# Two-layer graph network on one core: dilation loads and comparison re-staggered, ends of the second network's layers cut into smaller steps

## The chip, the cores and the metric

The kernel runs on 1 core of a Trainium2 chip. The core has five instruction streams, each in order: TensorE (PE; its weight loads are shown as PEld), VectorE (DVE), ScalarE (ACT), GpSimd (POOL) and SyncE (SP, which here only issues DMAs). The metric is device time in microseconds (us), lower is better. Before the change the median of three runs is 2877.07 us (2874.56 to 2882.93).

## The reference, cut to what matters

There are 16 graphs of 1024 nodes with 128 features, and a dense symmetric weight matrix `adj` per graph. Two networks are applied in turn, each to relu(layernorm(x)), and each result is added to x.

```python
# first network, three layers of
h = h @ W + b
nh = h / max(norm(h), eps)
h = (adj * (nh @ nh.T)) @ h          # relu between layers

# second network
keep = dilate(adj > 0)               # for n in range(1024): one row after the other
#   num = row.sum(); sf = (num + 1) // 2 if num > 10 else 1
#   rm = row & (cumsum(row) % sf == 0); row n and column n lose rm
adj_d = adj * keep
# three layers of
agg = (adj_d @ x) / deg
out = agg @ Wr + x @ Wx + b
h = batchnorm(relu(out / norm(out)))  # statistics over all 16 graphs
# at the end
y = concat(h1, h2, h3) @ Wl + bl
```

Two things order the work. The dilation is sequential in rows. A batch norm of the second network needs every graph's result before any graph may enter the next layer.

## The kernel before, in words

**Stage A (about the first 1700 us): the first network, with the dilation beside it.** `layer0()` is a generator that emits the first network for pairs of graphs. For each row of 128x128 blocks, `Batch.products` (line 329) multiplies features with features into a PSUM tile `pg`, of which there are two (line 344), and VectorE multiplies `pg` by the block's weights into `ew` (lines 353 and 356). TensorE then transposes `ew` (line 373) and sums it with the features (lines 384 and 398). The natural blocks of `adj` come from DRAM into `nat` (two buffers, line 245) and are transposed by TensorE (line 260); the rest of a block row goes straight into `adjA` (line 253). Both are DMAs on SP's queue.

`dilation()` (line 545) is a second generator. A block is a group of 128 rows (index k) of half the graphs: BH = 8 patterns, one for each graph. `dilate` makes three generators for a block:

- `loads` (line 581): for each pattern, SP loads 128 rows of `adj` (tile `an`, two buffers, line 585). ScalarE makes a 0/1 pattern of them (lines 587 and 588). For k > 0, SP also loads what is kept of the earlier columns, transposed (tile `kl`, two buffers, line 591), and VectorE combines the two (line 594).
- `rounds` (line 621): a fixed number of small iterations, which finds for every row which ranks go.
- `scans` (line 725): for each pattern, VectorE's running sum gives ranks (line 740, tile `rank`, three buffers), ScalarE takes an absolute value of them in place (line 749), VectorE compares them with a radius (line 760, tile `kp`), and GpSimd's queue stores the result to DRAM (line 761).

The loads of the next block are emitted between the scans of the present one. The main loop (line 797) hands out pieces of `layer0` according to weights that the dilation yields. That makes a program order; the framework's scheduler then sorts each engine's instructions by priority in that order and its own estimates of readiness, and the engines run what it wrote in order. So an edit of the dilation also shifts neighbouring instructions of the first network.

At about 1569 us a branch (line 822) tests whether the fast dilation was exact; it is not taken here. The rest of the first network follows, up to about 1700 us.

**Stage B (about 1700 to 2140 us): the second network's first layer.** It masks `adj`, writes the masked matrix back to DRAM, and sums.

**Stage C (about 2140 us to the end): its layers 1 and 2, and the output.** For each graph, `start2` (line 1065) normalizes (`normed`, line 1050: one ScalarE instruction over 1024 columns), projects with Wr and Wx (`weighted`, line 848), and projects the layer before with its part of Wl into `acc` (`project`, line 1057). `Sums.add` then does the large sums (line 888). `norms` (line 926) makes the row norms of half a graph: four squares on ScalarE with a sum each (line 933), a root and a reciprocal (`inv_root`, line 152), and one scaling on GpSimd (line 938). `keep` (line 942) transposes the scaled half and adds it to the batch norm's statistics. After the last graph comes `batchnorm` (line 950), and no graph can enter the next layer before it. `residual` (line 1075) folds x and the output bias into `acc`. The output loop (line 1113) projects the last layer and writes the sum.

Of the kernel before, what the change touches and what calls it, by code (L numbers as in the profile page):

```python
# [9 lines left out]
F16 = mybir.dt.float16  # L10
I32 = mybir.dt.int32
AF = mybir.ActivationFunctionType
ALU = mybir.AluOpType
# [3 lines left out]
P = 128  # L17
# [29 lines left out]
def tile_adj_preln_d2(  # L47
# [152 lines left out]
    with ExitStack() as actx:  # L200
# [362 lines left out]
        def dilate(k, half, exact):  # L563
# [6 lines left out]
            def pattern(i):  # L570
                return patt[:, (at0 + i) % SLOTS, :]
# [7 lines left out]
            E = radius = shift = low = None  # L579

            def loads():
                for i in range(BH):
                    b = half * BH + i
                    an = poold.tile([P, N], F32, tag="an", name=f"an{nk}_{i}")
                    nc.sync.dma_start(an, adj[b, cols, :])
                    on = pattern(i)[:, 2 + k * P :]
                    nc.scalar.activation(on, an[:, k * P :], AF.Sign)
                    nc.scalar.activation(on, on, AF.Relu, accum_out=rest[:, i : i + 1])
                    if k:
                        pk = poold.tile([P, NCH - 1, P], F16, tag="kl", name=f"kl{nk}_{i}")  # L590
                        nc.sync.dma_start(
                            pk[:, :k, :].rearrange("p j q -> p (j q)"), keep_d[b][: k * P, cols], transpose=True
                        )
                        nc.vector.scalar_tensor_tensor(
                            pattern(i)[:, 2 : 2 + k * P],
                            an[:, : k * P],
                            0.0,
                            pk[:, :k, :].rearrange("p j q -> p (j q)"),
                            ALU.is_gt,
                            ALU.mult,  # L600
                            accum_out=left[:, i : i + 1],
                        )
# [122 lines left out]
            def scans():  # L725

                i = 0
                while i < BH:
                    at_ = (at0 + i) % SLOTS
                    n = min(BH - i, SLOTS - at_)  # L730
                    here = patt[:, at_ : at_ + n, diag]
                    nc.vector.tensor_tensor(here, here, E[:, i : i + n, :], ALU.subtract)
                    i += n
                ranks = {}
                for i in range(BH + 1):
                    if i < BH:

                        pt = pattern(i)
                        ranks[i] = rank = poold.tile([P, N], F16, tag="rank", bufs=3, name=f"rank{nk}_{i}")
                        nc.vector.tensor_tensor_scan(rank, pt[:, 1 : N + 1], pt[:, 2:], 0.0, ALU.add, ALU.add)  # L740
                        yield True, 2.5
                    if i == 0:
                        continue

                    i -= 1
                    b = half * BH + i
                    pt, rank = pattern(i), ranks.pop(i)
                    tc.keep_in_program_order(
                        nc.scalar.activation(  # L749
                            rank, rank, AF.Abs, bias=shift[:, i : i + 1], scale=1.0 if exact else -1.0  # L750
                        )
                    )
                    kp = poold.tile([P, N], F16, tag="kp", name=f"kp{nk}_{i}")
                    if exact:
                        nc.vector.tensor_scalar(
                            kp, rank, low[:, i : i + 1], radius[:, i : i + 1], ALU.max, ALU.not_equal
                        )
                        nc.vector.tensor_tensor(kp, kp, pt[:, 2:], ALU.is_ge)
                    else:
                        nc.vector.tensor_scalar(kp, rank, radius[:, i : i + 1], None, ALU.not_equal)  # L760
                    nc.gpsimd.dma_start(keep_d[b][cols, :], kp)
                    yield False, 0.8

# [17 lines left out]
        step0()  # L781
        batches[1].fetch()

        mi = pool1.tile([P, P], I32, tag="mi", name="mi")[:NB, :]
        nc.gpsimd.dma_start(mi, nodemask.rearrange("b (c p) -> (b c) p", p=P))
        mfl = pool1.tile([P, P], F32, tag="up", name="mfl")[:NB, :]
        nc.vector.tensor_copy(mfl, mi)
# [49 lines left out]
    with ExitStack() as bctx:  # L837
# [29 lines left out]
        class Sums:  # L867
# [55 lines left out]
                        ALU.add,  # L923
                    )

            def norms(self, h):

                nm, b = f"{self.l}_{self.b}_{h}", self.b
                hc = slice(h * CPH, (h + 1) * CPH)
                ss = pool2.tile([P, CPH], F32, tag="in_ss", name=f"ss_{nm}")  # L930
                for c in range(CPH):
                    n = h * CPH + c
                    nc.scalar.activation(  # L933
                        self.own[:, n, :], self.o[:, n, :], AF.Square, accum_out=ss[:, c : c + 1]
                    )
                rn = inv_root(pool2, ss, nm)
                nc.vector.tensor_tensor(rn, rn, mf[:, b, hc], ALU.mult)  # L937
                nc.gpsimd.tensor_tensor(  # L938
                    self.o[:, hc, :], self.o[:, hc, :], rn.unsqueeze(2).to_broadcast([P, CPH, D]), ALU.mult
                )  # L940

            def keep(self, h):

# [21 lines left out]
        with kctx, ExitStack() as c1:  # L965
# [42 lines left out]
            def follow():  # L1008
                nonlocal last
                s, q, aT = behind.pop(0)  # L1010
                s.add(q, aT)
                if q == CPH + 1:
                    s.norms(0)
                if q == NCH - 1:
                    s.norms(1)
                    last = s

            then = ahead1
# [30 lines left out]

        def normed(l, b, ab):  # L1050
            hT = pool2.tile([P, NCH, P], F32, tag="hT2", name=f"hT2_{l}_{b}")
            nc.scalar.activation(  # L1052
                hT.rearrange("p c q -> p (c q)"), hR[:, b, :], AF.Identity, bias=ab[:, 1:2], scale=ab[:, 0:1]
            )
            return hT

        def project(l, b, hT):

            for h in range(NHALF):
                pp = ps_sm.tile([P, CPH, P], F32, tag="sm", name=f"pp_{l}_{b}_{h}")  # L1060
                for c in range(CPH):
                    nc.tensor.matmul(pp[:, c, :], lhsT=hT[:, h * CPH + c, :], rhs=wl[:, l, :], start=True, stop=True)  # L1062
                yield h, pp, acc[:, b, h * CPH : (h + 1) * CPH, :]

        def start2(l, b):
            hT = normed(l, b, ab)
            got = Sums(l, b, hT, CPH, 0, ps_a)
            for h, pp, a in project(l - 1, b, hT):
                if l == 1:
                    nc.scalar.activation(a, pp, AF.Copy)  # L1070
                else:
                    nc.vector.tensor_tensor(a, pp, a, ALU.add)
            return got

        def residual(b):

# [9 lines left out]
        for l in (1, 2):  # L1086
            last = None
            then = start2(l, 0)
            for b in range(B):
                now = then  # L1090
                for q in range(NCH):
                    aT = row_of(q, f"{l + 1}_{b}")
                    nc.sync.dma_start(aT, adT_d[b][q])
# [11 lines left out]
                        now.norms(0)  # L1105
                    if q == NCH - 2 and b == B - 1:
                        now.keep(0)
                now.norms(1)
                last = now
            last.keep(1)  # L1110
            ab = batchnorm(l)

        for b in range(B):
            y = pool2.tile([P, NCH, D], F32, tag=("o", "own")[b % 2], name=f"y_{b}")
# [66 lines left out]
```

## Time and profile before

| | us |
|---|---|
| median of three runs | 2877.07 |
| the profiled execution's own time | 2874.98 |
| its span, first to last instruction | 2873.2 |
| TensorE busy | 2659.3 (93% of the span) |
| VectorE busy | 1939.7 (68%) |
| ScalarE busy | 1426.0 (50%) |
| GpSimd busy | 473.7 (16%) |
| mean granted TensorE clock | 0.981 |

The profile is one execution. A line such as `PE pg L344 <- DVE ew L356: 63.5, 51, 3.8` means that TensorE's instructions of line 344, which write `pg`, were late 51 times, 63.5 us in total and 3.8 us at the longest, and that a VectorE instruction of line 356 ended the wait. In a list in order of time, the first number is the start, the second the duration, and a bracket holds the idle time of that engine before it and what ended it. A matmul with 32-bit operands is recorded as two matmuls.

### The profile page before, as it was taken

The page shows a single profiled execution, that of the slowest core. Times are in us where ns is not written, and L with a number is a line of the kernel's source. Part 1 is how long each engine was busy: PE and PEld are TensorE (multiplying, and loading weights), DVE is VectorE, ACT ScalarE, POOL GpSimd, SP SyncE. Part 2 cuts the span into 40 slices and gives each one's busy share as a digit, 9 for nine tenths or more (in the row PEclk, how much of TensorE's full clock was granted, in tenths as well). Part 3 has the DMA queues.
Part 4 walks back from the last instruction along what each step waited for, and adds up shares of the span by engine and source line. Part 5 has one row for each costly group of instructions (what it writes and reads, how often), then busy time and mean ns, then how long its engine had stood idle before and what let it go on. Part 6 is the DMA issues. An engine that isn't in the chain of part 4 may idle for free. (4 is left out here: it accounts for less than half of the span.)

```text
span 2873.2 us, 51953 instructions
## 1 busy us (share of the span) xinstructions
PE 2659.3 (93%) x18803; PEld 2199.0 (77%) x18803; DVE 1939.7 (68%) x4913; ACT 1426.0 (50%) x4100; POOL 473.7 (16%) x619
## 2 busy tenths in 40 slices
PE   6999998999999998989998998999989999899997
PEld 4666666666666666666676778898879999899996
DVE  3778778778878778789877467677762333356565
ACT  6767557557556556556455333333333433333334
POOL 3112112112011111112111012222220010010102
PEclk9999999999999999999999999999999999999998
DMA  9447247248366476286253249999985665577764
GB/s 287 130 139 236 77 155 236 86 137 247 87 186 178 99 199 191 80 257 191 55 190 115 75 168 380 379 401 401 397 333 191 202 213 202 183 236 229 237 230 134
DMA packets 382233, 585.22 MB, mean 204 GB/s; under 512 B 85200, under 2 KB 266448, under 8 KB 381968
## 3 DMA queue, kind: packets, MB, share of 16 engines
q1 hardware_dynamic: 343280, 425.28, 47.2%
q0 software_dynamic: 38688, 156.53, 14.5%
q8 instruction: 151, 2.47, 0.4%
q14 instruction: 114, 0.93, 0.1%
HBM read 403.44 MB, written 163.58 MB: 197 GB/s over the span
## 5 line engine op out<-in xcount | busy, mean ns | idle before, releaser
L888 PE MATMUL agg<-hw,aT 128*128 128x128 f32 (+1 forms) x6144 | 744.4, 277 | 8.2 <-DVE aT L985 7.3
L888 PEld LDWEIGHTS agg<-hw,aT 128*128 128x128 f32 x6144 | 713.6, 193 | 13.4 <-DVE aT L985 9.7
L344 PE MATMUL pg<-nhT 128*128 128x512 f32 (+3 forms) x1152 | 460.2, 502 | 69.5 <-DVE ew L356 65.5
L384 PE MATMUL po<-ew,hS 128*128 128x512 f32 (+3 forms) x1152 | 458.4, 501 | 8.7 <-ACT hTo L407 5.4
L356 DVE TENSOR_TENSOR ew<-pg,adjA 128x768 f32<-128x768 f32 (+3 forms) x528 | 423.2, 825 | 5.8 <-PE pg L344 5.7
L398 PEld LDWEIGHTS po<-ew,hS 128*128 128x128 f32 x2688 | 338.4, 193 | 40.3 <-issue 37.8
L398 PE MATMUL po<-ew,hS 128*128 128x128 f32 x2688 | 365.3, 277 | 1.2 <-ACT ew L374 1.2
L374 ACT ACTIVATE ew<-gt 128x512 f32<-128x512 f32 (+1 forms) x480 | 209.2, 465 | 247.8 <-PE gt L373 237.6
L344 PEld LDWEIGHTS pg<-nhT 128*128 128x128 f32 x1152 | 189.0, 194 | 164.8 <-issue 120.9
L740 DVE TENSOR_TENSOR_SCAN rank<-patt 128x1024 f16<-128x1024 f16 x128 | 295.0, 2316 | 0.9
L384 PEld LDWEIGHTS po<-ew,hS 128*128 128x128 f32 x1152 | 197.9, 195 | 100.8 <-issue 66.4
L373 PEld LDWEIGHTS gt<-ident,ew 128*128 128x128 f32 x1344 | 168.3, 143 | 100.2 <-issue 72.1
L353 DVE TENSOR_TENSOR ew<-pg,adjA 128x128 f32<-128x128 f32 x384 | 107.6, 280 | 184.9 <-PE pg L344 142.8
L938 POOL TENSOR_TENSOR o<-o,rn 128x512 f32<-128x512 f32 x96 | 111.4, 1160 | 646.6 <-DVE rn L937 627.7
L373 PE MATMUL gt<-ident,ew 128*128 128x128 f32 x1344 | 212.7, 276 | 4.9 <-PEq L822 2.4
L860 PE MATMUL pw<-wrx,hT 128*128 128x256 f32 x768 | 179.5, 388 | 10.5 <-ACT hT L1052 9.7
L862 DVE TENSOR_TENSOR own<-pw,bs 128x256 f32<-128x256 f32 x192 | 81.3, 424 | 156.9 <-ACT hw L861 156.8
L860 PEld LDWEIGHTS pw<-wrx,hT 128*128 128x128 f32 x768 | 145.0, 194 | 32.6 <-ACT hT L1052 10.5
L933 ACT ACTIVATE own<-o 128x128 f32<-128x128 f32 x384 | 114.4, 300 | 104.1 <-DVE o L917 104.0
L1003 ACT ACTIVATE aT<-pta 128x512 f32<-128x512 f32 (+3 forms) x160 | 71.1, 466 | 187.7 <-PE pta L1002 164.2
L749 ACT ACTIVATE rank<-rank,fin 128x1024 f16<-128x1024 f16 x128 | 146.7, 1151 | 30.8 <-DVE rank L740 30.2
L321 POOL TENSOR_TENSOR hS<-hN,rn 128x1024 f32<-128x1024 f32 x48 | 97.2, 2025 | 372.4 <-DVE rn L157 265.9
(165 smaller groups left out, 3910.5 us busy)
## 6 DMA issues: line engine op xcount, KB each, us to landing
an<-in_adj_dram SPq DMA_DIRECT2D x128, 512.0 KB, 4.4
keep<-kp POOLq DMA_DIRECT2D x128, 256.0 KB, 2.9
kb<-keep SPq DMA_DIRECT2D x128, 256.0 KB, 5.6
aT<-adT SPq DMA_DIRECT2D x32, 960.0 KB, 4.7
aT<-adT SPq DMA_DIRECT2D x32, 832.0 KB, 4.6
aT<-adT SPq DMA_DIRECT2D x32, 704.0 KB, 4.2
aT<-adT SPq DMA_DIRECT2D x32, 576.0 KB, 3.4
xb<-in_x_dram SPq DMA_DIRECT2D x31, 512.0 KB, 4.9
```

Of the source, the lines that this page charges most:

```text
L344: nc.tensor.matmul(pg[:, :n, :].rearrange("p c q -> p (c q)"), lhsT=self.nhT[:, q * P : (q + 1) * P], rhs=self.nhT[:, (q + c) * P : (q + c ...
L356: nc.vector.tensor_tensor(both[0][:, :, off, :], pg[:, own:n, :].unsqueeze(1).to_broadcast([P, 2, n - own, P]), both[1][:, :, off, :], ALU ...
L373: nc.tensor.transpose(pt[:, i, :], ew[:, at + i, :], ident)
L374: nc.scalar.activation(ew[:, at : at + n, :], pt[:, :n, :], AF.Copy)
L384: nc.tensor.matmul(self.po[:, c * P : (c + n) * P], lhsT=self.hS[:, q, :], rhs=ew[:, c - q : c - q + n, :].rearrange("p c q -> p (c q)"), ...
L398: nc.tensor.matmul(self.po[:, q * P : (q + 1) * P], lhsT=self.hS[:, q + n, :], rhs=ew[:, NCH - 1 - q + n, :], start=False, stop=closes and ...
L740: nc.vector.tensor_tensor_scan(rank, pt[:, 1 : N + 1], pt[:, 2:], 0.0, ALU.add, ALU.add)
L749: nc.scalar.activation(rank, rank, AF.Abs, bias=shift[:, i : i + 1], scale=1.0 if exact else -1.0)
L860: nc.tensor.matmul(pw[:, i, :], lhsT=hT[:, 2 * h + i, :], rhs=wrx[:, l, :], start=True, stop=True)
L888: nc.tensor.matmul(self.place(c), lhsT=aT[:, blk, :], rhs=self.hw[:, source, :], start=source == 0 and c % self.ga == 0, stop=ends(c, source),
L933: nc.scalar.activation(self.own[:, n, :], self.o[:, n, :], AF.Square, accum_out=ss[:, c : c + 1])
L938: nc.gpsimd.tensor_tensor(self.o[:, hc, :], self.o[:, hc, :], rn.unsqueeze(2).to_broadcast([P, CPH, D]), ALU.mult)
```

## The change

Five edits, and one of buffers:

1. In `loads`, the two DMAs of a pattern are issued one pattern ahead of the instructions that use them. The numbers of buffers of `an` and `kl` stay at two.
2. In `scans`, the comparison (`kp`) of a pattern is put one scan later than its absolute value; the absolute value stays where it was. `rank` gets a fourth buffer. A small tile `mi`, used once at the start, is moved into the slot of another tile (`T`).
3. In `norms` for the second half of the last graph of each layer (`soon`), two of the four squares go to VectorE, and the scaling goes from GpSimd to four VectorE instructions.
4. `normed` of graph 0 is split into four ScalarE instructions of 256 columns.
5. In layers 1 and 2, the last graph's projection into `acc` is taken from its `start2` and put after the layer's sums, before the last `keep`; it is added to `acc` after `batchnorm`. In layer 2 the addition is eight instructions that also apply the mask, where before it was two, since `residual` has by then run.

```diff
             def loads():
-                for i in range(BH):
+                got = {}
+
+                def get(i):
                     b = half * BH + i
                     an = poold.tile([P, N], F32, tag="an", name=f"an{nk}_{i}")
                     nc.sync.dma_start(an, adj[b, cols, :])
-                    on = pattern(i)[:, 2 + k * P :]
-                    nc.scalar.activation(on, an[:, k * P :], AF.Sign)
-                    nc.scalar.activation(on, on, AF.Relu, accum_out=rest[:, i : i + 1])
+                    pk = None
                     if k:
                         pk = poold.tile([P, NCH - 1, P], F16, tag="kl", name=f"kl{nk}_{i}")
                         nc.sync.dma_start(
                             pk[:, :k, :].rearrange("p j q -> p (j q)"), keep_d[b][: k * P, cols], transpose=True
                         )
+                    got[i] = an, pk
+
+                get(0)
+                for i in range(BH):
+                    if i + 1 < BH:
+                        get(i + 1)
+                    an, pk = got.pop(i)
+                    on = pattern(i)[:, 2 + k * P :]
+                    nc.scalar.activation(on, an[:, k * P :], AF.Sign)
+                    nc.scalar.activation(on, on, AF.Relu, accum_out=rest[:, i : i + 1])
+                    if k:
                         nc.vector.scalar_tensor_tensor(
...
                 ranks = {}
-                for i in range(BH + 1):
+                for i in range(BH + 2):
                     if i < BH:
                         pt = pattern(i)
-                        ranks[i] = rank = poold.tile([P, N], F16, tag="rank", bufs=3, name=f"rank{nk}_{i}")
+                        ranks[i] = rank = poold.tile([P, N], F16, tag="rank", bufs=4, name=f"rank{nk}_{i}")
                         nc.vector.tensor_tensor_scan(rank, pt[:, 1 : N + 1], pt[:, 2:], 0.0, ALU.add, ALU.add)
                         yield True, 2.5
-                    if i == 0:
+                    if 1 <= i <= BH:
+                        tc.keep_in_program_order(
+                            nc.scalar.activation(ranks[i - 1], ranks[i - 1], AF.Abs,
+                                bias=shift[:, i - 1 : i], scale=1.0 if exact else -1.0))
+                    if i < 2:
                         continue
-                    i -= 1
-                    pt, rank = pattern(i), ranks.pop(i)
-                    tc.keep_in_program_order(nc.scalar.activation(rank, rank, AF.Abs, ...))
+                    ii = i - 2
+                    pt, rank = pattern(ii), ranks.pop(ii)
...
-                        nc.vector.tensor_scalar(kp, rank, radius[:, i : i + 1], None, ALU.not_equal)
+                        nc.vector.tensor_scalar(kp, rank, radius[:, ii : ii + 1], None, ALU.not_equal)
                     nc.gpsimd.dma_start(keep_d[b][cols, :], kp)
                     yield False, 0.8
...
-            def norms(self, h):
+            def norms(self, h, soon=False):
                 for c in range(CPH):
-                    nc.scalar.activation(self.own[:, n, :], self.o[:, n, :], AF.Square, accum_out=ss[:, c : c + 1])
+                    o, sq = self.o[:, h * CPH + c, :], self.own[:, h * CPH + c, :]
+                    if soon and c >= CPH // 2:
+                        nc.vector.scalar_tensor_tensor(sq, o, 1.0, o, ALU.mult, ALU.mult, accum_out=ss[:, c : c + 1])
+                    else:
+                        nc.scalar.activation(sq, o, AF.Square, accum_out=ss[:, c : c + 1])
                 rn = inv_root(pool2, ss, nm)
                 nc.vector.tensor_tensor(rn, rn, mf[:, b, hc], ALU.mult)
-                nc.gpsimd.tensor_tensor(...)
+                if soon:
+                    for c in range(CPH):
+                        o = self.o[:, h * CPH + c, :]
+                        nc.vector.tensor_scalar(o, o, rn[:, c : c + 1], None, ALU.mult)
+                else:
+                    nc.gpsimd.tensor_tensor(...)
...
         def normed(l, b, ab):
-            nc.scalar.activation(hT.rearrange("p c q -> p (c q)"), hR[:, b, :], AF.Identity, ...)
+            n = NCH if b else 2
+            for c in range(0, NCH, n):
+                nc.scalar.activation(hT[:, c : c + n, :]..., hR[:, b, c * P : (c + n) * P], AF.Identity, ...)
...
         def start2(l, b):
             hT = normed(l, b, ab)
             got = Sums(l, b, hT, CPH, 0, ps_a)
+            if b == B - 1:
+                return got, hT
             for h, pp, a in project(l - 1, b, hT):
...
-                now.norms(1)
+                now.norms(1, soon=b == B - 1)
                 last = now
+            late = list(project(l - 1, B - 1, hT))
             last.keep(1)
             ab = batchnorm(l)
+            for h, pp, a in late:
+                if l == 1:
+                    taken(0, pp, a)
+                    continue
+                for c in range(CPH):
+                    n = h * CPH + c
+                    nc.vector.scalar_tensor_tensor(
+                        a[:, c, :], pp[:, c, :], mf2[:, B - 1, n : n + 1], a[:, c, :], ALU.mult, ALU.add)
```

In the first layer (stage B), `norms(1, soon=s.b == B - 1)` is called in the same way.

## The prediction

> **What bounds the kernel now.** I read busy time by stretches, then the waits of TensorE, VectorE and SyncE's DMA queue, then the timeline at one stall and at one boundary of layers. By stretches (`x` counts instructions):
>
> ```profile
> core 0: us, PE busy (x) PEld busy (x) DVE busy (x) ACT busy (x) POOL busy (x), PEclk, DMA share, GB/s
> 100.00:1570.00 1470.00, 1356.03 (x8539) 989.68 (x8537) 1172.07 (x2782) 878.20 (x2350) 242.24 (x309) 0.99 0.52 155
> 2160.00:2480.00 320.00, 319.43 (x2640) 313.04 (x2638) 98.46 (x311) 118.04 (x413) 32.23 (x31) 1.00 0.63 210
> 2480.00:2498.00 18.00, 8.66 (x44) 7.28 (x43) 8.67 (x26) 7.31 (x19) 1.04 (x1) 0.72 0.14 54
> 2819.00:2873.20 54.20, 34.39 (x262) 32.47 (x261) 30.78 (x110) 30.46 (x60) 11.21 (x9) 0.84 0.51 156
> ```
>
> TensorE is the bound everywhere: 92% in the dilation stretch, over 99% inside a layer of the second part. An edit can pay only where TensorE stands still: 1470 - 1356 = 114 us up to 1570, and some 9 us at each of three boundaries. (About 1700 to 2140 the DMA share is 1.02; only the last norms there are touched.) What TensorE waits for in the dilation stretch (us in total, times, longest):
>
> ```profile
> PE pg L344 <- DVE ew L356: 63.5, 51, 3.8
> ...
> PE pt_a L260 <- DMA nat<-in_adj_dram: 7.3, 5, 4.6
> ```
>
> All waits that VectorE ends sum to 90.1 us. Same view for VectorE, then for SyncE's DMA queue over the run:
>
> ```profile
> DVE ew L353 <- PE pg L344: 108.3, 76, 4.5
> DVE kp L760 <- ACT rank L749: 49.4, 40, 4.5
> ...
> DVE patt L594 <- DMA kl<-keep: 24.8, 12, 4.2
> ```
>
> ```profile
> SPq L585 <- DVE patt L594: 450.3, 61, 56.9
> ```
>
> VectorE loses 49.4 us to the comparison and 24.8 to the kept rows (edits 2 and 1); yet it also waits 108.3 for TensorE, so only part of that reaches the bound. One comparison that does, on VectorE and then TensorE:
>
> ```profile
> 1063.12 0.49 DVE L760 TENSOR_SCALAR kp<-rank,fin 128x1024 f16<-128x1024 f16 x1 [4.33 <-ACT rank L749]
> 1063.64 2.29 DVE L740 TENSOR_TENSOR_SCAN rank<-patt 128x1024 f16<-128x1024 f16 x1
> 1065.85 0.27 DVE L353 TENSOR_TENSOR ew<-pg,adjA 128x128 f32<-128x128 f32 x1
> 1066.03 0.94 DVE L356 TENSOR_TENSOR ew<-pg,adjA 128x768 f32<-128x768 f32 x1
> ```
>
> ```profile
> 1067.12 0.88 PE L344 MATMUL pg<-nhT 128*128 128x384 f32 x2 [0.67 <-DVE ew L356]
> ```
>
> VectorE stood 4.33 us; TensorE paid 0.67. The boundary from layer 1 to 2:
>
> ```profile
> 2482.62 0.17 DVE L154 TENSOR_SCALAR ss<-ss 128x4 f32<-128x4 f32 x1
> 2483.59 1.04 POOL L938 TENSOR_TENSOR o<-o,rn 128x512 f32<-128x512 f32 x1 [4.33 <-DVE rn L937]
> 2484.68 1.11 PE L165 MATMUL pt_r<-ident,o 128*128 128x128 f32 x4 [4.49 <-POOL o L938]
> ...
> 2489.35 2.37 ACT L1052 ACTIVATE hT<-hR,bn_ab 128x1024 f32<-128x1024 f32 x2 [0.81 <-DVE bn_ab L961]
> 2490.64 5.16 PE L860 MATMUL pw<-wrx,hT 128*128 128x256 f32 x16 [4.85 <-ACT hT L1052]
> 2495.63 1.95 PE L1062 MATMUL pp<-wl,hT 128*128 128x128 f32 x16
> ```
>
> TensorE stands 4.49 us until the last sums are normed and scaled and 4.85 us until the batch norm and `hT`: a serial chain, in which every microsecond counts.
>
> **The dilation stretch, edits 1 and 2.** To see which VectorE stall stands behind each of TensorE's 90.1 us, I followed VectorE back from the instruction that ended each wait to its last idle time that TensorE itself had ended, and shared the wait over the stalls between. Result: 11.7 us go back to comparisons that waited for the absolute value, 8.0 us to waits for kept rows, 57.1 us to bursts without any stall (one scan of 2.3 us, or several small instructions, between two `ew` multiplies), the rest (13.3) to other waits.
>
> - *Comparison one scan later.* In 40 waits the excess over one scan (2.3 us) is 7.9 us, from eight of them: the longer distance hides 41.5 of 49.4 us (84%). Gain 11.7 x 0.84 = 9.8 us. It adds no instruction; keeping `rank` one scan longer is paid with its fourth buffer. After a half's last scan one more comparison stands beside its neighbour with no scan between: 0.49 us, within the burst estimate below.
> - *Loads one ahead.* The kept-row DMA is issued earlier only if its buffer is free, and the count stays two. Row `SPq L585 <- DVE patt L594` says the queue already stands at the next load 61 times until VectorE has released the buffer; one kept-row load, issued at 261.92 us, its buffer freed at 259.7, landed at 266.46, and VectorE waited 3.72: there nothing moves. I take a quarter of the 8.0 us: -2 (from 0 to -8).
> - *Bursts.* Summing the row durations of what stands between two `ew` multiplies in each kernel's order of instructions, the time by which bursts exceed 5 us falls from 126.0 to 113.3, and beyond 6 us from 79.0 to 67.9: 11 to 13 us shorter. TensorE pays 57.1 of the 227.8 us beyond 3.5 us (a quarter): -3.
> - *The queues passed.* Each early issue is two DMAs on SyncE's queue (`an` 512 KB, the kept rows), ahead of what stood there: the next graph's `nat` and `adjA` loads and `xb`. If the load has to wait for its buffer, all behind it waits too; 450 us of such waiting exists already, and TensorE's direct loss to `nat` is 7.3 us. With as many loads moved by one pattern, I let that grow by 40%: +3 (0 to +28, the slow rival). GpSimd's `keep` writes come one scan (2.3 us) later, against 112 patterns whose reader is a whole column block away. `mi`, used once: nothing.
>
> Sum: -9.8 - 2 - 3 + 3 = -11.8.
>
> **The boundaries, edits 3 to 5.**
>
> - *Squares and scaling.* Four squares on ScalarE take 4 x 0.300 us (mean row, `own<-o`) in a row; two beside two on VectorE (0.341 each, the mean of L917's instructions of that size) save some 0.6, though VectorE's pair also stands behind its last sums: I count 0.4. Scaling on GpSimd costs 1.04 us plus a handover each way; `pt_r` could start after the first of four VectorE pieces of about 0.2 (small VectorE rows are 0.16 to 0.18), the last 0.8 after the start: 0.6 saved. Together -1.0 at the first boundary. The price: while GpSimd scaled, a VectorE step of the next chain (L154) took 0.84 us instead of 0.17 at 2142, which also goes.
> - *First piece of `hT`.* 1024 columns take 1.24 us on ScalarE; a line of 1.055 ns a column + 0.16 us, through it and the squares' 128 columns (0.297), gives 0.43 for 256. The first `pw` matmul starts 1.24 - 0.43 = 0.81 earlier; the four pieces end at 1.73, 0.5 later, but each 256-column piece feeds four matmuls (1.3 us at the half rate, 0.32 each), more than ScalarE needs. -0.81 at each of three boundaries.
> - *Projection moved.* Sixteen records, 1.95 us (L1062), leave a stretch that is over 99% busy and go where TensorE would stand 4.49 us for `pt_r`: -1.95 in layers 1 and 2. Its cover is that stand; without it the edit is worth nothing. `pp` is then added late. In layer 1 by two ScalarE copies of 0.60 us (L1070), which the order puts among the last squares, in front of what the sums wait for: up to +0.7 on the chain. In layer 2 by eight VectorE multiply-adds of 0.34 in place of two additions of 0.69: +1.3 us of VectorE, and in the order of instructions one stands before `ss`, one each before the root's reciprocal, the mask's product and the scaling, one between the statistics and their aggregate: four on the chain, +1.3, of which it was standing idle at one or two: +0.9 to +1.3.
>
> First boundary: -1.0 - 0.8 = -1.8. Second: -1.0 + 0.7 - 0.8 - 1.95 = -3.05. Third: -1.0 + 1.3 - 0.8 - 1.95 = -2.45. Sum -7.3.
>
> [...] The row shows the clock: granted 0.72 over 2480 to 2498; in the trace it falls to half 2 to 3 us after TensorE goes idle and stays there 13.65, 10.24 and 13.65 us at the three boundaries, all multiples of 3.41. [...] I keep -7.3: the projection fills 1.95 us of the first stand and so shortens the idle time. Range -3 to -11.
>
> **The sum.** -11.8 - 7.3 = -19.1. On the profiled execution, own time 2874.98 (span 2873.2 and 1.8 around it), that is 2855.9; the median of the runs is 2877.07, 2.1 higher, so 2877.07 - 19.1 = **2858**.
>
> **Rivals.**
>
> - *Waits only move.* VectorE waits 108.3 us for TensorE; what it saves at comparisons may appear there, and 57 of 90 us lie in bursts, which hardly change. Against: the 1063 stall did reach TensorE. Then only the boundaries pay: -6 to -7, 2870.
> - *More than its share.* VectorE arriving early at each scan lets `pg` buffers build a lead that covers later bursts: if a third of the 57.1 (-19) goes with comparisons and kept rows in full (-11.7 - 8.0), less 3 back, the stretch gives -36 and the time is about 2877 - 36 - 7 = 2834 to, at half that extra, 2843: 2840.
> - *Slower: SyncE's queue.* Place: a load at the queue's head one pattern earlier, waiting for the combine at L594 to free its buffer, with `nat` and `adjA` behind it. For: 450.3 us of that wait exist, and `nat` already stalls TensorE by up to 4.6. Price: the reordering touches 112 patterns with kept rows; at 0.3 us of TensorE each, +34, and with the other -16.8 -5 (-7.3 boundaries, -9.8 comparisons, no more than -2 and -3): 2877 + 34 - 19 = 2892. It decides once TensorE pays over 22.1 / 112 = 0.2 us a pattern (without the +3 counted above).
> - *It doesn't do what it says.* With two buffers, edit 1 may move no landing; then -2 and +3 fall away, 2857: the same forecast.
>
> **How the numbers follow.** Likeliest (2858) 0.44; waits only move (2870) 0.18; more (2840) 0.18; slower (2892) 0.20. A measurement of this kernel can tell about 0.3%, 8.6 us: faster means below 2868.4, slower above 2885.7. Faster: nearly all of the first (0.40), all of "more" (0.18), a little of "only move" (0.02): 0.60. Same: 0.04 + 0.15 + 0.02 = 0.21. Slower: the queue's 0.18 and 0.01 besides: 0.19. Range 2838 to 2884: from "more" with its larger end left out, to the queue rival's beginning; the likeliest one's own range is 2848 to 2868.
>
> **What would show it.** In the dilation stretch: TensorE busy stays near 1356 us of work while the waits of `pg` on `ew` fall from 63.5 to about 50; the waits of `kp` on `rank` fall from 49.4 to about 8; those of `patt` on kept rows stay near 20; those of `pt_a` on `nat` do not exceed 10. At the boundaries: `pt_r` after about 3.5 us and no GpSimd instruction before it; `L1062` in front of `pt_r`; first `pw` 0.8 us after `hT` is begun; half rate for 10 to 14 us as before. Wrong if `nat` waits or SyncE's waits at the load grow by tens of microseconds that TensorE pays, or if VectorE's wait for TensorE takes up what the comparisons gave.

## The result, and the profile after

The changed kernel takes as long as the one before: 2876.80 us against 2876.66 (medians of 20 runs each), ratio 0.9997 with a 95% interval of 0.9985 to 1.0009. Forecast were 2858 us and faster. The profiled execution has a span of 2867.5 us against 2873.2; with single runs from 2864 to 2886 us that difference is nothing by itself.

Busy time by stretches of the kernel after (columns as before: stretch, length, then busy us of PE, PEld, DVE, ACT, POOL, granted clock, DMA share, GB/s). The last two stretches are set 4.0 and 5.5 us earlier than before, as the boundaries came earlier:

```profile
100.00:1570.00 1470.00, 1354.40 (x8550) 993.12 (x8549) 1174.21 (x2786) 881.63 (x2354) 243.38 (x309) 0.98 0.52 156
2160.00:2480.00 320.00, 318.94 (x2634) 312.36 (x2632) 100.95 (x322) 118.95 (x417) 32.28 (x31) 1.00 0.64 212
2476.00:2494.00 18.00, 11.06 (x53) 9.16 (x52) 9.75 (x34) 8.30 (x19) 0.79 (x1) 0.72 0.23 80
2813.50:2867.50 54.00, 35.68 (x282) 33.69 (x282) 33.84 (x126) 30.52 (x59) 10.70 (x9) 0.91 0.51 156
```

In the dilation stretch TensorE does no more than before in the same 1470 us (1354 against 1356 us busy), and its granted clock reads 0.98 where it read 0.99 (over all runs 0.9800, against 0.9817 in the runs of the kernel before that stand beside the experiments). At the boundary it stands 2.4 us less. What TensorE, VectorE and SyncE's queue wait for (us in total, times, longest; the first two from 100 to 1570 us, the third over the run):

```profile
PE pg L344 <- DVE ew L356: 73.8, 50, 3.9
...
PE pt_a L260 <- DMA nat<-in_adj_dram: 2.2, 2, 1.4
```

```profile
DVE ew L353 <- PE pg L344: 107.7, 80, 4.7
DVE kp L777 <- ACT rank L757: 38.9, 26, 4.6
DVE patt L605 <- DMA kl<-keep: 35.6, 19, 4.9
```

```profile
SPq L587 <- DVE patt L605: 506.7, 72, 57.2
...
SPq L591 <- DMA keep<-kp: 36.5, 10, 9.7
```

The wait for the comparison fell by only 10.5 of 49.4 us, the wait for kept rows rose by 10.8, and TensorE's wait for `ew` rose from 63.5 to 73.8. The loads of kept rows now wait 36.5 us until the *writes* they read have landed; that was 3.2 us before. One such stall, on VectorE and then on TensorE:

```profile
681.43 0.69 DVE L605 SCALAR_TENSOR_TENSOR patt<-an,kl 128x512 f16<-128x512 f32 x1 [4.10 <-DMA kl<-keep]
682.05 0.08 DVE L605 DVE_READ_ACCUMULATOR patt<-an,kl 128x1 f32 x1
682.05 0.28 DVE L353 TENSOR_TENSOR ew<-pg,adjA 128x128 f32<-128x128 f32 x1
682.25 1.81 DVE L356 TENSOR_TENSOR ew<-pg,adjA 128x768 f32<-128x768 f32 x2
```

```profile
683.35 0.99 PE L344 MATMUL pg<-nhT 128*128 128x256 f32 x2 [2.82 <-DVE ew L356]
```

VectorE stood 4.10 us at a combine, with the multiplies that free `pg` behind it, and TensorE paid 2.82. (In the same trace the granted clock is then at half for 3.41 us, from 683.56.) The boundary from layer 1 to 2:

```profile
2477.57 1.95 PE L1094 MATMUL pp<-wl,hT 128*128 128x128 f32 x16
...
2481.23 0.87 DVE L961 TENSOR_SCALAR o<-o,rn 128x128 f32<-128x128 f32 x4
2481.67 0.82 PE L165 MATMUL pt_r<-ident,o 128*128 128x128 f32 x4 [2.15 <-DVE o L961]
...
2486.05 2.08 ACT L1080 ACTIVATE hT<-hR,bn_ab 128x256 f32<-128x256 f32 x4 [0.81 <-DVE bn_ab L986]
2486.70 6.63 PE L877 MATMUL pw<-wrx,hT 128*128 128x256 f32 x16 [4.21 <-ACT hT L1080]
2493.39 1.95 PE L1094 MATMUL pp<-wl,hT 128*128 128x128 f32 x16
```

The projection fills TensorE's first stand, which shrinks from 4.49 to 2.15 us, the scaling has no GpSimd in it, and the second stand is 4.21 instead of 4.85. So the boundaries came earlier as forecast, and the dilation stretch took the gain back.

For the dilation stretch I made the same walk as in the prediction (each TensorE wait that VectorE ends is followed back along VectorE and shared over the stalls between; the rest is a burst), from 30 to 1569 us of each profile, and counted how many of the 112 kept-row loads are issued less than 5 us after the write they need has landed. Before and after: all such waits 90.1 and 105.0; comparisons 11.7 and 5.6; combines (their kept rows, their `adj` rows or issue) 8.0 and 22.7; bursts 57.1 and 64.8; loads on the heels of their writes 4 and 25.

### The profile page after: what moved, and what is told of

It reads as the page before. It is cut to its first block, busy times and chain, and to the rows that moved or that the text cites. A ratio compares the mean times of both kernels' runs of the same rounds, so it can differ in the third digit from the quotient of the medians.

```text
span 2867.5 us, 51991 instructions
## 1 busy us (share of the span) xinstructions
PE 2655.8 (93%) x18803; PEld 2201.2 (77%) x18803; DVE 1946.0 (68%) x4943; ACT 1426.6 (50%) x4097; POOL 473.0 (16%) x616
## 3 DMA queue, kind: packets, MB, share of 16 engines
q0 software_dynamic: 38688, 156.53, 14.5%
## 5 line engine op out<-in xcount | busy, mean ns | idle before, releaser
L344 PE MATMUL pg<-nhT 128*128 128x512 f32 (+3 forms) x1152 | 456.1, 500 | 82.3 <-DVE ew L356 73.8
L778 POOL DMA_DIRECT2D keep<-kp x128 | 70.8, 554 | 535.3 <-DVE kp L777 466.9
```

The costliest lines, as they stand in the source:

```text
L344: nc.tensor.matmul(pg[:, :n, :].rearrange("p c q -> p (c q)"), lhsT=self.nhT[:, q * P : (q + 1) * P], rhs=self.nhT[:, (q + c) * P : (q + c ...
```

## The experiments

**Which part pays, which loses.** The edits were put into the kernel before one group at a time.

```diff
  tail_only        edits 3, 4, 5
  dilation_only    edits 1, 2, with the small tile's move
  loads_only       edit 1
  lag_only         edit 2, with the fourth rank buffer and the small tile's move
```

> The kernel before with edits 3 to 5 alone. If the boundaries pay in every run what they paid in the profile of after (10.72 us from the last squares to the first matmul of layer 1 became 9.45; 340.09 from there to layer 2 became 336.55; 338.84 to the output layer became 337.29), the time falls by some 6.5 us: ratio 0.9977, 2870 us, and the loss of the same size lies in the dilation stretch. If the gain was that one execution's alone: ratio 1.000.

Measured 0.9983 (0.9970 to 0.9996), 2872.15 us against 2878.48. From the first matmul of layer 1 to layer 2 it took 336.12 us, and 336.89 from there to the output layer; from the first `pt_r` after the first layer to layer 1's first matmul 6.44 us against 7.81 to 7.83 in the kernels without these edits. The gain is real and lies where it was forecast.

> Edits 1 and 2 alone. If they lose what edits 3 to 5 gain: +6.5 us, ratio 1.0023. If they do nothing and the boundaries' gain isn't real: 1.000. As forecast (-11.8): 0.9959.

1.0017 (1.0007 to 1.0026), 2883.80: edits 1 and 2 cost some 5 us, and 5 less 5 is the result.

> Edit 1 alone. Theory B (two buffers: a load still starts only when the combine two patterns before has read its buffer, and the combine is now placed earlier on VectorE's queue than its rows can land): VectorE's waits for kept rows rise from 24.8 to some 33 us, the TensorE waits that go back to them from 8.0 to 14 or more, time +3 to +6 us. Theory W (the kept rows are read before the write of the block before has landed, which needs both edits): this alone gives 0 +-2 us, and fewer than 6 of the 112 loads issue within 1 us of their write's landing (2 before, 12 after). Rival of the prediction (head of SyncE's queue): TensorE's waits for nat grow over 10 us.

1.0003 (0.9990 to 1.0017), and the trace is that of before: kept rows 24.7 us, their share of TensorE's waits 9.2, two loads within 1 us of their write, `nat` 8.9. Theory B and the rival fall for this edit, which does nothing; theory W is right so far.

> Edit 2 alone. Theory B: VectorE's wait for the absolute value falls from 49.4 to under 39 us, what of TensorE's waits goes back to it from 11.7 to about 5, kept rows stay near 25 us, time -3 to -6 us. Theory W: as much, 0 to -6. Rival (comparisons without a pause behind scans make longer bursts on VectorE): the bursts' part rises from 57 to 65 us and the time is +0 to +4.

1.0006 (0.9995 to 1.0017). VectorE's waits in this kernel:

```profile
DVE kp L766 <- ACT rank L746: 40.3, 26, 4.6
DVE patt L594 <- DMA kl<-keep: 32.8, 18, 4.9
```

That is the picture of after: comparisons' share of TensorE's waits 5.7, combines 19.2, bursts 63.3, 25 loads within 5 us of their write. Edit 2 alone makes the picture, so theory W with its need of both edits is wrong. Theory B had the kept rows stay near 25 us (32.8 measured) and the time fall by 3 to 6, and is wrong too; the rival with its longer bursts (65 us forecast) comes nearest.

**Is the stall at the kept rows the price?** The build decides the order of each engine's instructions; here each combine is held behind all VectorE instructions written before it.

```diff
-nc.vector.scalar_tensor_tensor(pattern(i)[:, 2 : 2 + k * P], ...)
+tc.keep_in_program_order(nc.vector.scalar_tensor_tensor(pattern(i)[:, 2 : 2 + k * P], ...))
```

> Edit 2 alone, and each combine of the kept rows (the VectorE instruction at the end of a load) pinned behind all VectorE instructions written before it. Theory O (edit 2 lets the build's order put the combines further ahead on VectorE's queue, 7.1 us behind the landing of their rows at the median where it was 11.8, so they stand in front of ready work): VectorE's waits for kept rows fall from 41.0 to under 25 us, TensorE's share of them from 19.2 to under 10, and the time is 3 to 8 us below edit 2 alone (2872 to 2877). Theory P (the pauses at the comparisons used to hide the loads; whatever the order, what is saved there is waited for at the rows): kept rows stay at 35 to 45 us and the time within 3 us of edit 2 alone.

> The kernel before with the combines pinned, no other edit. Theory O: kept rows' waits fall from 24.8 to under 15 us and the time by 0 to 4 us, comparisons' waits staying near 50. Theory P: comparisons' waits rise by what the rows' fall, time unchanged.

With edit 2: 1.0012 (0.9995 to 1.0030); without: 1.0007 (0.9992 to 1.0022). No combine waits at all in either, so theory O is right about the order; but neither is faster. In time theory P is right for lag_pin, though its reason does not hold in pin_only: there VectorE's wait at comparisons took up only 4.1 of the 24.8 us that the rows lost (49.4 to 53.5). TensorE's waits in the pinned kernel without edit 2:

```profile
PE pg L344 <- DVE ew L356: 50.6, 42, 3.8
PE pw L293 <- ACT adjA L261: 12.2, 5, 3.5
PE po L384 <- ACT hTo L407: 9.1, 14, 1.8
```

Waits that VectorE ends fell from 90.1 to 72.3 us, those that ScalarE ends rose from 24.8 to 49.2, and all waits together went from 125.1 to 127.0. The wait moved to another engine. So the stall at the rows, though TensorE is seen to pay for it, is not by itself what the time depends on.

**How much is the accident of order?** The two streams of work are interleaved by weights. The weight of a comparison was changed and nothing else; the instructions are the same, their order is not.

```diff
-                    yield False, 0.8
+                    yield False, 0.85        (and 0.75, 0.90)
```

> A control: the kernel before with the weight of a comparison in the interleaving of the two streams 0.85 in place of 0.8; the same instructions in another order. If the dilation stretch's waits depend on the accident of the order as much as on the edit, TensorE's waits that VectorE ends move by several us from 90.1 and the time by up to 5 us; if not, both stay within 2 us, and what edit 2 did is its own.

> The kernel before with the weight 0.75 and no edit. If 0.85 gained because a comparison was costed too low, this loses: ratio about 1.003. If the order alone scatters the time: anywhere within 0.3% either way, TensorE's waits by VectorE within 80 to 100 us.

> The kernel before with the comparison's weight 0.90. The fourth order without edit 2; the others stood at 1 (0.80), 0.9972 (0.85) and 0.998 (0.75). Within 0.997 to 1.001; TensorE's waits by VectorE 79 to 92 us as in those.

0.9972 (0.9961 to 0.9983), 0.9980 (0.9969 to 0.9991) and 0.9923 (0.9898 to 0.9948); the first and the last lie outside what was expected. A weight is worth up to 22 us, more than the whole forecast, and both directions gain: the order of the kernel before was a poor draw. Then the same weights with edits 1 and 2:

> Edits 1 and 2 with the comparison's weight 0.85 (the order that made the kernel before 8.8 us faster). If edits 1 and 2 cost their 4.9 us in any order: ratio about 0.9989 (2873.5). If that cost is an accident of one order: anything from 0.997 to 1.002, and TensorE's waits that VectorE ends anywhere from 85 to 105 us (99 to 105 in the three orders with edit 2 so far, 88 to 92 without it).

> Edits 1 and 2 with the weight 0.75. If they cost 4.9 us in any order, this stands some 5 us above the kernel before with 0.75 (the run beside it). If by accident of the order, the two differ by an amount with no fixed sign.

> Edits 1 and 2 in the order of weight 0.90. If their cost has a fixed sign, this stands 5 to 13 us above the run beside it, as in the three orders before; if the three were chance, within 4 us of it or below. TensorE's waits by VectorE 8 to 15 us above the run beside it in the first case, with the bursts' part 6 or more above.

1.0019 (1.0009 to 1.0029), 1.0003 (0.9992 to 1.0013), 0.9999 (0.9985 to 1.0014). Beside the same weight without the edits that is 0.47%, 0.23% and 0.77% more, and 0.17% at the weight 0.80: one sign in four orders, though of no fixed size. At 0.90 the difference is 22 us, beyond the 5 to 13 forecast.

**Which part of edit 2?** It has two: the later place of the comparison and the fourth `rank` buffer.

```diff
  rank_four_only   (no edit 2; the small tile's move)
-ranks[i] = rank = poold.tile([P, N], F16, tag="rank", bufs=3, ...)
+ranks[i] = rank = poold.tile([P, N], F16, tag="rank", bufs=4, ...)
  lag_rank_three   (edit 2; the small tile's move)
-ranks[i] = rank = poold.tile([P, N], F16, tag="rank", bufs=4, ...)
+ranks[i] = rank = poold.tile([P, N], F16, tag="rank", bufs=3, ...)
```

> A fourth rank buffer and the small tile's move, no edit else. If the cost of edit 2 comes from scans running further ahead into the fourth buffer: bursts' part from 57 to over 61 us, time +2 to +5 us. If it comes from the comparison's later place: traces as before (bursts 57, comparisons 11 to 12), ratio 1.000.

> Edit 2 alone with three rank buffers: a scan cannot start before the comparison three patterns back, so scans can't run ahead. If the fourth buffer is the cause, bursts 57 and the time at or below the kernel before; if the comparison's place is, bursts 61 to 65 and kept rows' part 15 to 20 us as in edit 2 alone, ratio 1.0006 to 1.002.

1.0014 (1.0003 to 1.0025) and 0.9941 (0.9918 to 0.9963). The buffer alone, without a single comparison moved, gives most of the trace of after: bursts 64.3, combines 17.2, 27 loads within 5 us of their write. Not all of it: the comparisons' share of TensorE's waits stays at 11.4, and falls to 5.7 only with the later comparison. TensorE's largest wait, VectorE's waits, and a wait of SyncE's queue, in that kernel:

```profile
PE pg L344 <- DVE ew L356: 71.9, 52, 3.8
```

```profile
DVE kp L760 <- ACT rank L749: 39.5, 30, 3.9
DVE patt L594 <- DMA kl<-keep: 30.7, 18, 3.2
```

```profile
SPq L591 <- DMA keep<-kp: 38.3, 11, 5.4
```

Even the fall of VectorE's wait at comparisons (49.4 to 39.5) comes with the buffer, without the later comparison. What it does is seen on VectorE's timeline. The kernel before at the start of a block's scans (only scans and the comparison are shown):

```profile
340.07 4.46 DVE L740 TENSOR_TENSOR_SCAN rank<-patt 128x1024 f16<-128x1024 f16 x2
...
346.94 2.28 DVE L740 TENSOR_TENSOR_SCAN rank<-patt 128x1024 f16<-128x1024 f16 x1
...
359.43 0.49 DVE L760 TENSOR_SCALAR kp<-rank,fin 128x1024 f16<-128x1024 f16 x1 [0.68 <-ACT rank L749]
```

The same place with a fourth buffer:

```profile
342.02 4.47 DVE L740 TENSOR_TENSOR_SCAN rank<-patt 128x1024 f16<-128x1024 f16 x2
...
348.88 2.28 DVE L740 TENSOR_TENSOR_SCAN rank<-patt 128x1024 f16<-128x1024 f16 x1
...
353.54 2.28 DVE L740 TENSOR_TENSOR_SCAN rank<-patt 128x1024 f16<-128x1024 f16 x1
...
363.45 0.48 DVE L760 TENSOR_SCALAR kp<-rank,fin 128x1024 f16<-128x1024 f16 x1
```

Three scans run before the first comparison, then four; so it is in 10 of the 16 blocks, where the kernel before never has more than three. From a pattern's scan to its comparison it is 24.2 us at the median before and 30.9 with the buffer; with edit 2 and three buffers it is 24.7. The writes of `keep` are later by that, and the loads of the next blocks follow them. That is what was forecast for the fourth buffer, and not what was forecast for the comparison's place. The size of the gain with three buffers (16 us) was in neither.

**Does that hold in the whole kernel?** After with `bufs=3` for `rank`, at both weights.

> The changed kernel with three rank buffers in place of four, nothing else. If the fourth buffer is what took the gain back: the 0.9941 of edit 2 with three buffers and the boundaries' 0.0017 to 0.0026 add up to 0.9915 to 0.9924, 2852 to 2855 us, faster than both kernels; TensorE's waits by VectorE under 92 us, bursts' part under 55, fewer than 10 loads within 5 us of their write's landing. If 0.9941 was an accident of that order: 0.995 to 0.998.

> The same with the comparison's weight 0.90. Without edits 1 and 2 that order stands at 0.9923, with them and four buffers at 0.9999. With three buffers and the boundaries' gain: 0.990 to 0.992 if edit 2 itself adds nothing to a good order, 0.985 if its gain of 16 us adds in any order, near 0.998 if the loss is edit 2's and not the buffer's.

0.9914 (0.9896 to 0.9932), 2853.33 us, and 0.9937 (0.9920 to 0.9954), 2860.77. The first is faster than both kernels, by 0.8% over after; the second lies between what two of the theories gave. TensorE's and VectorE's waits in the first:

```profile
PE pg L344 <- DVE ew L356: 63.0, 51, 3.3
```

```profile
DVE kp L777 <- ACT rank L757: 50.7, 36, 4.4
DVE patt L605 <- DMA kl<-keep: 21.5, 10, 4.5
```

Kept rows and `ew` are back near before; so are the comparisons, at 50.7 us. With three buffers edit 2 does not shorten the wait it aims at. Its 0.9941 lies inside what the order alone gives (0.9923 to 1), and at the weight 0.90 the edits with three buffers (0.9937, of which some 0.2% is the boundaries') are no better than none (0.9923). That the later comparison is worth anything in time is not shown.

**The boundaries, taken apart, and the sum with another order.**

> Edits 3 and 4 alone, the projection left in its old place. From the last squares to the first matmul: layer 1 as in after (9.45 us). From first matmul to first matmul: layer 1 to 2 some 338.5 us (340.09 before, 336.55 after), layer 2 to the output some 337.3 (338.84 and 337.29): the projection gives 1.95 us in layer 1 and, with its late additions on the chain, nothing in layer 2. Forecast as on record: 1.95 less 0.7 in layer 1, 1.95 less 1.3 in layer 2, so 337.8 and 337.9. If it were the whole gain: 340 and 339.

0.9987 (0.9969 to 1.0004); 338.96 and 338.89 us from first matmul to first matmul. The projection gives what is between that and tail_only: 2.8 and 2.0 us, both more than forecast (1.25 and 0.65). These are single executions; the same two distances scatter by 2.0 and 1.5 us among the kernels without edits 3 to 5. In the time of the whole kernel the projection is not seen: 2872.12 us without it, 2872.15 with it.

> Edits 3 to 5 with the weight 0.85, no edit of the dilation: the two gains lie in different stretches and should add, -4.9 to -7.5 at the boundaries and -8.8 before them: ratio 0.9945 to 0.9953, 2861 to 2863 us, faster than both kernels. If the reordered stretch ends so that the second part is met in another state: 0.997.

0.9938 (0.9917 to 0.9960), 2864.85 us. The sum would be 0.9955, just inside the interval; with after_rank_three it fits that gains at the boundaries and in the dilation stretch add.

The stretch before 1569 us in the kernels without edits 3 to 5 (us of TensorE's waits that VectorE ends, and of these bursts, combines, comparisons; loads within 5 us of their write; us of all of TensorE's waits; how many of them are over 2 us). The last column is the granted clock, the mean of all runs of the kernel and not of the profiled one alone:

| kernel | rank buffers | ratio | waits | bursts | combines | comparisons | loads | all waits | over 2 us | clock |
|---|---|---|---|---|---|---|---|---|---|---|
| before | 3 | 1 | 90.1 | 57.1 | 8.0 | 11.7 | 4 | 125.1 | 14 | 0.9817 |
| loads_only | 3 | 1.0003 | 91.4 | 57.4 | 9.2 | 12.1 | 4 | 132.2 | 15 | 0.9814 |
| pin_only | 3 | 1.0007 | 72.3 | 42.4 | 0 | 6.2 | 2 | 127.0 | 16 | 0.9820 |
| reorder_only_75 | 3 | 0.9980 | 79.1 | 48.4 | 1.6 | 18.3 | 6 | 122.3 | 19 | 0.9804 |
| reorder_only | 3 | 0.9972 | 82.2 | 52.7 | 8.6 | 12.6 | 3 | 121.6 | 15 | 0.9822 |
| lag_rank_three | 3 | 0.9941 | 87.8 | 48.9 | 7.8 | 19.1 | 7 | 120.8 | 15 | 0.9837 |
| reorder_only_90 | 3 | 0.9923 | 83.3 | 44.7 | 5.9 | 15.8 | 2 | 112.5 | 11 | 0.9833 |
| rank_four_only | 4 | 1.0014 | 106.8 | 64.3 | 17.2 | 11.4 | 27 | 134.7 | 21 | 0.9815 |
| lag_only | 4 | 1.0006 | 99.0 | 63.3 | 19.2 | 5.7 | 25 | 128.4 | 23 | 0.9789 |
| dilation_only | 4 | 1.0017 | 101.1 | 60.9 | 21.8 | 5.6 | 25 | 130.9 | 23 | 0.9787 |
| lag_pin | 4 | 1.0012 | 77.5 | 56.6 | 0 | 5.6 | 2 | 126.0 | 20 | 0.9786 |
| reorder_dilation_75 | 4 | 1.0003 | 89.5 | 57.5 | 15.3 | 7.4 | 33 | 128.7 | 18 | 0.9805 |
| reorder_dilation | 4 | 1.0019 | 96.0 | 65.7 | 11.1 | 11.1 | 26 | 134.5 | 20 | 0.9799 |
| reorder_dilation_90 | 4 | 0.9999 | 93.1 | 56.9 | 6.8 | 9.8 | 25 | 128.4 | 20 | 0.9796 |

Every kernel with four buffers stands between 0.9999 and 1.0019, those with three between 0.9923 and 1.0007. The comparisons' column does not go with the ratio; bursts do better, if not alone (pin_only). Four pairs differ in the buffer and in little else: rank_four_only and before (also the small tile's move), lag_only and lag_rank_three, after and after_rank_three, reorder_dilation_90 and after_rank_three_90 (only the second has the boundaries' edits, for which 0.17% is taken off). The kernel with the fourth buffer is longer by 0.14%, 0.65%, 0.83% and 0.45%: one sign. But each pair is also two draws of the order, which alone gave up to 0.77%, so the sign is shown better than the sizes.

**Where the time goes.** In all 20 profiles the span, less TensorE's idle time and less half of the time in which it works at half clock, is 2612 to 2621 us, while the spans go from 2847 to 2881; so these two terms make nearly all of the difference between kernels. From after to after_rank_three the span fell by 20.4 us: 14.5 us less idle time, and 6.0 us less lost at half clock. With four buffers more of TensorE's waits are long: 18 to 24 are over 2 us, against 11 to 19 with three. Up to 1569 us each of the 16 stretches at half clock in the profile of before (54.6 us) and of the 15 in that of after (64.9) begins within 5 us of the start of a TensorE wait of 1.6 us or more. The buffer alone adds idle time (10.0 us over the span) and leaves the mean clock where it was (0.9815), for all its 21 long waits; so their number does not settle the clock. With edit 2 as well the clock falls, to 0.9789 in lag_only: 1 less the clock, times the span, is then 61 us a run in place of 53. So edit 2 with four buffers takes 8 us off the waits that VectorE ends in rank_four_only (106.8 to 99.0), and some 7 more are lost at half clock; the times are alike.

## Why the prediction was wrong

1. **The fourth buffer, counted at nothing.** The step that failed: "It adds no instruction; keeping `rank` one scan longer is paid with its fourth buffer." The buffer is not only cover but a change of the order: scans go one further ahead, and alone it costs 0.14% (4 us; 1 to 7). Taking it out of the changed kernel gives 0.8% (24 us). The sum also has no term for the granted clock in this stretch (the clock was read at the boundaries alone): over all runs it was 0.9787 in dilation_only against 0.9816 in the kernel before beside it, 8 us more a run by the measure above.
2. **Comparisons, -9.8.** Their share of TensorE's waits fell by 6.1, and that did need the later comparison (11.4 with the buffer alone); VectorE's own wait falls as much through the buffer alone (39.5 us in rank_four_only, 40.3 in lag_only). "The longer distance hides 41.5 of 49.4 us" took the order as given: the build chose a new one, in which 26 comparisons still wait 38.9 us, up to 4.6.
3. **Kept rows, -2 from the loads.** Edit 1 gave 0, the rival "it doesn't do what it says": with two buffers a load still starts when the combine two patterns back is done (SyncE's queue waits 451.3 us for that in loads_only, 450.3 before). The total went the other way (+14.7 us at combines in TensorE's waits), for a reason under "the queues passed": "against 112 patterns whose reader is a whole column block away". A block away in the code is not far in time: four loads had less than 5 us before, and 25 have it after. The pins show that this wait is not the price by itself.
4. **Bursts, -3.** TensorE's waits at them rose by 7.7. Summed from the two traces, the time by which bursts exceed 5 us does fall, from 130.3 to 123.8, by half of the forecast. But the quarter that TensorE pays was a share of the time beyond 3.5 us, and that stays (241.4 and 240.5); the share itself rose to 27%. That TensorE's lead over VectorE is smaller when a burst comes would explain it, but is not shown.
5. **SyncE's queue, +3.** Its sign was wrong: the wait for `nat` fell from 7.3 to 2.2 us (with edit 1 alone, to which the +3 belongs, it is 8.9; with edit 2 alone 2.5). The slow rival did not occur. (Its sum has a slip: without the +3 the other terms are -17.1 - 5 = -22.1, not -16.8 and not -19, which gives 2889 and not 2892 us; the 22.1 / 112 is right, and nothing hung on it.)
6. **Boundaries, -7.3.** Right as a sum. From the first `pt_r` to layer 1 it is -1.4, and from there to the end it is 717.05 us in tail_only and 717.38 in after, against 722.66 to 725.04 in the fourteen kernels without these edits: about -6. In time tail_only has -4.9 us (-8.6 to -1.2). That the sum came out is luck in part, for the terms were mis-sized against each other: in the traces the projection is worth 4.8 and not 1.9, edits 3 and 4 some 3 and not 5.4. Where the projection's surplus comes from is seen in the clock. At the second and third boundary together the clock is at half for 23.89 us in each of the fifteen kernels without the moved projection, tail_no_projection among them, and for 17.07 or 20.48 in the five with it. Half of the difference, 1.7 to 3.4 us, is about the surplus. The forecast "half rate for 10 to 14 us as before" was wrong: over the three boundaries it is 37.55 us before and 27.31 after.
7. **The clock at the boundaries, read and not counted.** In layer 2 the first matmul starts 3.5 us earlier relative to layer 1, but the 16 records of `pw` then take 6.46 us up to TensorE's next work instead of 4.99. The granted clock reads 0.54 over them (2486.70 to 2493.16) where it read 0.71 before (2490.64 to 2495.63): they run for 5.92 us at the half clock in place of 2.94, and half of that difference, 1.5 of the 3.5, is given back there. In kernels with unchanged boundaries the same 16 take from 4.99 to 6.43 (lag_only), so that loss need not be the edits'. Over the three boundaries the traces give about -7.5, close to the -7.3 added up from the rows, and for the reason for which it was kept: the projection fills part of the stand (4.49 us became 2.15), and the clock is at half for a shorter time (27.31 us in place of 37.55). The range of -3 to -11 was the author's estimate.

"Waits only move" came nearest, with 2870 for the case in which the dilation stretch gives nothing; it gave a loss of 5. What in VectorE's order makes TensorE's waits longer with four buffers stays open: neither the stall at the rows (removed in lag_pin, time unchanged) nor the comparisons explain it, and the bursts go with it without having been tried alone. Also open is whether edit 2 with three buffers gains anything beyond one more draw of the order.

## What to carry to other kernels

Where a build chooses the order, an added buffer is an edit of its own: it lets a producer run ahead, and what it delays (here the comparison and the write that a later load reads) must be costed; try it alone, and try the edit without it. A wait removed on an engine that is not the bound is worth only what the bound pays over *all* its waits: pinning took 18 us of VectorE's away, and ScalarE's came in their place. Nor is the total of the waits enough: in the traces of before and after every stretch at half clock up to 1569 us began beside a long wait, so read the granted clock of all runs as well. Before a gain of 0.5% is put down to an edit, reorder the kernel without it and see what that alone does.

## What the hardware runs showed unexpectedly

The same instructions in another interleaving differed by 22 us (0.77%), and two executions of one order differ as well: the value that ends the stretch is computed at 1568.5 us in the profile of before and at 1575.3 in that of tail_only, whose code up to there is the same. The granted clock accounts for it: 54.6 us at half rate up to there against 64.8, which is 5.1 us lost, and 1.7 us more idle time. Over the 210 runs of the kernel before that stand beside the experiments, a run that loses 1 us more by its mean clock (1 less the clock, times the span) is longer by 0.95 us (correlation 0.83). And the share of TensorE's waits that VectorE ends went from 99 us in lag_only to 72 in pin_only while all of TensorE's waits stayed at 128 and 127 us.
